# Spreading layers 1 and 2 of a group over 1.9 groups of differences, and writing the sorted degrees behind the differences of a PSUM tile

## The chip, the cores and the metric

The kernel runs on one core of one Trainium2 chip. A core has a matrix engine (TensorE, PE in the profile; its weight loads are listed as PEld), a vector engine (DVE), an activation engine (ACT), a general engine (POOL) and a queue that issues transfers (SP). The metric is the device time of one execution in microseconds, lower is better. Matmul results land in PSUM, which has eight banks of 512 fp32 values in each of 128 partitions.

## What is computed

The input is 128 graphs of 128 nodes with 64 features each, and a dense weighted adjacency matrix for each graph, about one entry in eight of it non-zero. Four layers follow each other. Each normalises the features, takes the positive part and adds what its block gives.

```
layer 0:  h[j,k] = relu(x[j] W1a + (x[j] - x[k]) W1b + b1)      for each edge j,k
          x += (sum over k of h[j,k]) W2 + degree[j] * b2
layer 1:  three times  h = relu(adj (h W + b)),  then  x += h Wout + bout
layer 2:  y = (adj h + h) W + b, each row divided by its norm,
          then normalised over all graphs and nodes (mean, variance), x += relu(y)
layer 3:  m = adj h;  x += tanh([h, m] W1 + b1) W2 + b2
```

Layer 0 is the large one: a difference and a positive part of 192 columns for every edge.

## The kernel before

The graphs are worked in 32 groups of G = 4. For layer 0 the nodes of a graph are sorted by their number of neighbours, and the neighbours of a node are numbered. One **task of differences** handles one neighbour number of all nodes of a group: a one-hot matrix (`oh` or `ohn`, made by DVE at lines 542 and 547) picks the neighbour's projected features by matmul, and the result is added to what node j itself gives. A group has 20 tasks: 12 for near neighbours (4 matmuls each) and 8 for others (12 each, three bf16 parts), in a fixed order, all of 128x192.

A task goes round three engines. ACT fills a difference tile in PSUM with `psort`, the node's own part (`fill`, line 561). PE adds the differences to it (line 569; every matmul is recorded under line 103). DVE adds the positive part to an accumulator in SBUF (lines 580 and 584; one task of a group, line 582, is ACT's). There are three difference tiles, `blks[0]` to `blks[2]`, of two banks each, and task t uses tile t mod 3. A tile's two banks have 512 columns each, of which 384 are used by differences. The columns behind them hold, in tiles 0 and 1, sums for layer 2 (`ysum`, `ysq`). The other two banks are a pool, from which every other matmul result takes one by turns (`bank`).

Beside the differences of group g two other kinds of work are woven in, written as Python generators that yield between steps:

- `prepare(g + 1)`: transposes the adjacency, numbers neighbours, sorts nodes (`lower`, `fro`, `to`, `to_b`), projects the features (`q`), stores and reloads them in another layout, and makes `psort`. It computes the degree of each node and the number of neighbours beyond the near ones (`degs`, two columns of bf16), and sorts them with four matmuls into tile `ps_deg` (lines 495 to 498). DVE makes `empty` and `spare_n` from it (lines 510 and 511); ACT uses `empty` in line 526, and `spare_n` is read at the end.
- `after_layer0(g - 1)`: the end of layer 0 (`layer0_end`: `ps_sA`, `ps_sB`, `ps_o`), `layer1` (a chain of `ps_ah`, `ps_ag`, `ps_pr` with a copy by ACT between each two) and the first half of `layer2_norm` (`ps_ga`, `ps_pr`, then norms, and sums over nodes into `ysum`). For group 29 it ends with `first_mean`, a mean over the groups so far; line 773 then subtracts it from `ys` of every group.

What sets the order of the work is a plan at build time. Each generator is held with the number of its units (15 and 26), the number done, and the number of groups that it lasts: 0.8 for `prepare`, `LASTS` = 1.5 for `after_layer0`. After each half of a task the plan takes the generator that is most behind, and steps it while there is budget:

```
late, s = max(((s[2] * s[3] / (nyields * s[4]) - s[1], s) for s in side), key=lambda k: k[0])
if late <= 0 or (spent["us"] >= budget and late < LAG):
    break
```

`s[2]` are the units, `s[3]` the halves of tasks since its start, `nyields` the 40 halves of a group, `s[4]` the groups that it lasts. `spent` is the plan's own guess of PE's time and `PACE` what it allows for half a task. With 1.5, `after_layer0` of two groups are in work at once in the first half of each group, and one alone in the second half. What is not done when the last group's differences end (`side[0][0]`) is stepped in turn with the last group's own `after_layer0`. The framework that records the program then orders each engine's instructions and sets the waits, so an engine's order is close to the written one, but not the same. It sets waits on a PSUM tile so that instructions of different engines on it come one after the other.

Of the kernel before, what the change touches and what calls it, by code (L numbers as in the profile page):

```python
# [20 lines left out]
G = 4  # L21
# [26 lines left out]
N_PREPARE, N_AFTER = 15, 26  # L48
PACE, LAG = 0.88, 2.5
LATE = 18  # L50
LASTS = 1.5
PARTS = [2, 4, 6, 6, 6, 8]
AHEAD = 3
NBLK = 3
W = NP * H0


@with_exitstack
def tile_adj_preln_d4(ctx: ExitStack, tc: tile.TileContext, io, out: bass.AP):
    nc = tc.nc  # L60
    const = ctx.enter_context(tc.tile_pool(name="const", bufs=1))
    over = const.tile([1, 1], I32, name="over")
    with ExitStack() as inner:
        network(inner, tc, io, out, over=over)
    more = nc.values_load(over, min_val=0, max_val=P)
    with tc.If(more > 0):
        x1 = nc.dram_tensor("x1_dram", [io["x"].shape[0] // G, P, G, F], F32, kind="Internal").ap()
        with ExitStack() as inner:
            dense_layer0(inner, tc, io, x1)
        with ExitStack() as inner:  # L70
            network(inner, tc, io, out, x1=x1)


def network(ctx, tc, io, out, over=None, x1=None):
# [7 lines left out]
    NG = B // G  # L82
# [10 lines left out]
    def spend(w, n, dtype):  # L93
        f32 = dtype == F32
        kind = (f32, tuple(w.shape), n)
        m = w.shape[-1]
        one = max(0.026, 0.00043 * n) if not f32 else max(0.22, 0.0018 * n) * (0.5 if m == F and n == P else 1.0)
        spent["us"] += one + (0.045 if kind != spent["kind"] else 0.0)
        spent["kind"] = kind

    def matmul(o, w, x, **kw):
        spend(w, math.prod(x.shape[1:]), x.dtype)
        return nc.tensor.matmul(o, w, x, **kw)  # L103
# [111 lines left out]
    where, at = {}, 0  # L215
# [31 lines left out]
    blks = [ps_blk.tile([P, 1024], F32, tag=f"blk{i}", name=f"blk{i}") for i in range(NBLK)]  # L247
# [3 lines left out]


    ysum, ysq = (t.rearrange("p (a n) -> p a n", a=2)[0:G, :, W:512] for t in blks[0:2])
    for t in (ysum, ysq):
        nc.vector.memset(t, 0.0)


# [25 lines left out]
    def bank(name):  # L283
        return ps.tile([P, 512], F32, tag="ps", name=name)
# [116 lines left out]
    def prepare(g):  # L401
# [6 lines left out]
        a = loaded.pop(g)  # L408
# [18 lines left out]
        degs = edge.tile([P, G, 2], BF16, tag="degs", name="degs")  # L427
# [33 lines left out]
        to_b = once.tile([P, G, P], BF16, tag="to_b", name="to_b")  # L461
# [30 lines left out]
        for q in range(3):  # L492
            nc.sync.dma_start(near_n[g % 2][q * THIRD : (q + 1) * THIRD].rearrange("r t b n -> r t (b n)"), n_dram[g].rearrange("(t r) c -> r t c", t=3))
        yield
        pd = bank("ps_deg")
        for b in range(G):
            matmul(pd[:, 2 * b : 2 * b + 2], to_b[:, b, :], degs[:, b, :], start=True, stop=True)
        pdv = pd[:, 0 : 2 * G].rearrange("p (b q) -> p b q", q=2)

        num_r = edge.tile([P, G, P], BF16, tag="num_r", name="num_r")  # L500
        for i in range(LIKE):
# [1 line left out]
        m, n = len(SEGS) - LIKE, SEGS[LIKE]  # L503
# [194 lines left out]
    def after_layer0(g):  # L698
        if x1 is None:
            yield from layer0_end(g)  # L700
        else:
            nc.sync.dma_start(xs[g], x1[g])
            save_transposed(g, load_adj(g))
        yield
        yield from layer1(g)
        yield from layer2_norm(g)
        if g == NG - 3:
            first_mean()
# [8 lines left out]
    else:  # L717


        run(prepare(0))  # L720
        per = len(tasks) // NG
        nyields = 2 * per
# [7 lines left out]
        for g in range(NG):  # L730
            if g:
                side.append([after_layer0(g - 1), 0, N_AFTER, 0, LASTS])
            if g + 1 < NG:
                side.append([prepare(g + 1), 0, N_PREPARE, 0, 0.8])
            for t in range(g * per, (g + 1) * per):
                for _ in differences(t):
                    budget += PACE
                    for s in side:
                        s[3] += 1
                    while side:  # L740
# [3 lines that stand above are left out]
                        step = next(s[0], "end")  # L744
                        s[1] += 1 if step is None else step if step != "end" else 0
                        if step == "end":
                            side.remove(s)
                    budget = min(budget, spent["us"] + PACE)
            if g + 1 < NG:
                assert len(side) <= 1  # L750
# [115 lines left out]
    parts, at = [], 0  # L866
# [183 lines left out]
```

## Time and profile before

| | us |
|---|---|
| median of three runs | 1437.3 (1434.69 to 1447.62) |
| profiled execution | 1441.81 |
| its span, first to last instruction | 1440.0 |
| DVE, closing a task (line 584), 576 times | 545.8 busy, 951 ns each |
| ACT, filling a tile (line 561), 544 times with `psort`, 96 with `psort_r` | 437.4 and 77.6 busy, 808 ns each |
| PE, difference matmuls, 3072 and 1536 | 325.9 and 203.6 busy |

The profile is one execution, taken by the hardware profiler. "Busy" of an engine is the time in which at least one of its instructions was running; matmuls are pipelined, so that a matmul of 248 ns is followed by the next after 82 ns, and PE's busy time holds such tails. Line numbers are those of the kernel before. A group of instructions is named by its line, the tile that it writes and those that it reads, with buffer numbers left out: `blk<-q,oh` is a difference matmul. A wait is put down to the instruction that ended it.

The start takes about 79 us (group 0 has to be prepared before anything else), groups 1 to 31 end at 1279.6, and the rest is the end of layer 2 and all of layer 3.

### The profile page before, as it was taken

How to read it: one execution, taken by the hardware profiler on the slowest of the kernel's cores; microseconds unless marked ns; L12 is line 12 of the kernel's file. 1: busy time of each engine (PE TensorE's matmuls, PEld its weight loads, DVE VectorE, ACT ScalarE, POOL GpSimd, SP SyncE). 2: the span in 40 equal slices, each digit the busy share in tenths (PEclk: the TensorE clock that was granted, in tenths of full speed). 3: DMA queues.
4: the chain of work that ended last, by engine and by line, in shares of the span. 5: the costliest groups of instructions: out<-in, count | busy, mean ns of one | idle time of the engine just before them, and what ended most of it. 6: DMA issues, size and time to landing. Idle time of an engine off the chain costs nothing.

```text
span 1440.0 us, 29446 instructions
## 1 busy us (share of the span) xinstructions
PE 1278.7 (89%) x11124; PEld 981.7 (68%) x11124; DVE 1197.9 (83%) x2691; ACT 1004.1 (70%) x1883; POOL 175.4 (12%) x258
## 2 busy tenths in 40 slices
PE   3788999999999999999999999999999999995788
PEld 1567777777777777777777777776777777763566
DVE  7788888888888888888888888888888888874983
ACT  1677777777777777777777777777677777862783
POOL 3000000000000000000000000000000000003930
PEclk9799999999999999999999999999999999997899
DMA  4543222222222222222222222222222222200345
GB/s 106 132 111 89 66 81 81 80 76 79 80 73 73 78 70 71 68 59 81 81 81 74 80 74 80 73 73 71 60 63 78 74 73 73 74 9 8 82 118 128
DMA packets 108788, 110.97 MB, mean 77 GB/s; under 512 B 42895, under 2 KB 88220, under 8 KB 108636
## 3 DMA queue, kind: packets, MB, share of 16 engines
q1 hardware_dynamic: 108636, 109.00, 28.0%
q8 instruction: 89, 1.46, 0.4%
q14 instruction: 63, 0.52, 0.1%
HBM read 52.70 MB, written 35.29 MB: 61 GB/s over the span
## 4 chain that ended last, share of the span: by engine, by line
PE 63%; DVE 20%; ACT 13%; issue 4%; DMA 0%; POOL 0%; DVEq 0%; ACTq 0%; POOLq 0%
PE blk L103 22%; PE ps_pr L103 10%; PE ps_ag L103 7%; DVE acc L584 5%; PE ps_p L103 5%; ACT blk L561 5%; PE ps_ga L103 4%; PE ps_sB L103 2%; PE ps_q L103 2%; PE ps_sA L103 2%; PE ps_ah L103 2%; PE ps_hm L103 2%; PE ps_to L108 2%; DVE lower L441 1%; DVE fro L451 1%
## 5 line engine op out<-in xcount | busy, mean ns | idle before, releaser
L584 DVE SCALAR_TENSOR_TENSOR acc<-blk,acc 128x768 f32<-128x768 f32 x576 | 545.8, 951 | 133.6 <-PE blk L103 91.2
L561 ACT COPY blk<-psort 128x768 f32<-128x768 f32 x544 | 437.4, 808 | 122.0 <-DVE acc L584 115.1
L103 PE MATMUL blk<-q,oh 128*128 128x192 bf16 x3072 | 325.9, 248 | 27.3 <-ACT blk L561 21.4
L103 PEld LDWEIGHTS <-oh 128*128 128x128 bf16 x3072 | 261.0, 98 | 55.5 <-issue 52.4
L103 PE MATMUL blk<-near_q,ohn 128*128 128x192 bf16 x1536 | 203.6, 247 | 10.9 <-ACT blk L561 9.3
L103 PEld LDWEIGHTS <-ohn 128*128 128x128 bf16 x1536 | 129.8, 98 | 64.1 <-issue 41.1
L642 POOL TENSOR_TENSOR x<-x,t 128x256 f32<-128x256 f32 x32 | 23.7, 741 | 529.2 <-DVE t L641 512.7
L103 PEld LDWEIGHTS <-ones_b 3*128 3x128 bf16 (+2 forms) x312 | 29.1, 93 | 74.3 <-issue 67.6
L561 ACT COPY blk<-psort_r 128x768 f32<-128x768 f32 x96 | 77.6, 808 | 0.7 <-DVE acc L584 0.7
L103 PE MATMUL ps_pr<-g,dT 128*128 128x128 f32 x512 | 74.0, 287 | 0.0
L103 PEld LDWEIGHTS ps_pr<-g,dT 128*128 128x128 f32 x512 | 62.0, 191 | 15.1 <-issue 15.1
L103 PE MATMUL ps_ag<-adjT,msg 128*128 128x128 f32 x512 | 71.9, 283 | 0.1
L542 DVE TENSOR_SCALAR ohn<-near_n 128x1536 bf16<-128x1536 bf16 x128 | 70.6, 555 | 0.0
L103 PEld LDWEIGHTS ps_ag<-adjT,msg 128*128 128x128 f32 x512 | 62.1, 191 | 5.2 <-ACT msg L635 2.3
L298 ACT ACTIVATE sq<-xc 128x256 f32<-128x256 f32 x96 | 40.1, 417 | 32.1 <-DVE xc L295 32.1
L627 ACT ACTIVATE dT<-ps_ag 128x512 f32<-128x512 f32 x96 | 56.9, 593 | 3.4 <-PE ps_ag L103 2.1
L103 PE MATMUL ps_p<-wp,hs 128*128 128x384 f32 x128 | 59.1, 544 | 0.0
L103 PE MATMUL ps_sA<-fro,acc 128*128 128x128 f32 x256 | 53.7, 292 | 3.5 <-DVE acc L584 2.5
L103 PE MATMUL ps_q<-wq,hT 128*128 128x384 f32 x128 | 52.6, 535 | 4.2 <-ACT hT L325 1.1
L103 PE MATMUL ps_hm<-ident,h 128*64 128x128 f32 x248 | 41.8, 299 | 14.0 <-ACT h L841 14.0
L668 POOL TENSOR_TENSOR y<-y,nrm 128x256 f32<-128x256 f32 x32 | 19.8, 619 | 276.9 <-PE blk L103 261.2
L526 ACT ACTIVATE extra<-psort,empty 128x192 f32<-128x192 f32 x128 | 51.2, 450 | 0.0
(221 smaller groups left out, 2610.8 us busy)
## 6 DMA issues: line engine op xcount, KB each, us to landing
q_dram<-q SPq DMA_DIRECT2D x32, 567.0 KB
near_q<-q_dram SPq DMA_DIRECT2D x96, 189.0 KB
near_n<-n_dram SPq DMA_DIRECT2D x96, 126.0 KB
a<-in_adj_dram SPq DMA_DIRECT2D x32, 256.0 KB
adjT_dram<-adjT SPq DMA_DIRECT2D x32, 256.0 KB
adjT<-adjT_dram SPq DMA_DIRECT2D x32, 256.0 KB
psort_r<-psort SPq DMA_DIRECT2D x32, 228.0 KB
fro_r<-fro SPq DMA_DIRECT2D x32, 152.0 KB
```

The costliest lines, as they stand in the source:

```text
L103: return nc.tensor.matmul(o, w, x, **kw)
L108: return nc.tensor.transpose(o, x, i)
L298: nc.scalar.activation(sq, xc, AF.Square)
L441: nc.vector.tensor_tensor(lower, pk.rearrange("p (b n) -> p b n", n=P), key.unsqueeze(2).to_broadcast([P, G, P]), ALU.is_lt)
L451: nc.vector.tensor_scalar(flat(fro), pl, place_p, None, ALU.is_equal)
L526: nc.scalar.activation(of(extra, b), of(psort, b), AF.Relu, scale=empty[:, g, b : b + 1])
L542: nc.vector.tensor_scalar(oh.rearrange("p t b n -> p (t b n)"), near_n[g % 2].rearrange("p t b n -> p (t b n)"), float(i + 1), None, ALU.i ...
L561: nc.scalar.copy(columns(t), psorts[g][in_segments(n)])
L584: nc.vector.scalar_tensor_tensor(acc, o, 0.0, acc, ALU.max, ALU.add)
L627: nc.scalar.activation(flat(dT), pa, AF.Relu)
L642: nc.gpsimd.tensor_tensor(xt, xt, t, ALU.add)
L668: nc.gpsimd.tensor_tensor(y, y, over_f(nrm), ALU.mult)
```

## The change

The number of groups over which `after_layer0` is spread goes from 1.5 to 1.9. And the sorted degrees no longer take a bank of the pool: they are written into the columns behind the differences of tile 2, at a place of their own for each group (8 columns; 16 groups in each of the tile's two banks). Those columns are set to zero once, and the matmuls add to that instead of starting afresh (`start=False`). Nothing else changes.

```diff
-LASTS = 1.5
+LASTS = 1.9
...
     ysum, ysq = (t.rearrange("p (a n) -> p a n", a=2)[0:G, :, W:512] for t in blks[0:2])
-    for t in (ysum, ysq):
+    degs_at = blks[2].rearrange("p (a n) -> p a n", a=2)[:, :, W:512]
+    for t in (ysum, ysq, degs_at):
         nc.vector.memset(t, 0.0)
...
-        pd = bank("ps_deg")
-        for b in range(G):
-            matmul(pd[:, 2 * b : 2 * b + 2], to_b[:, b, :], degs[:, b, :], start=True, stop=True)
-        pdv = pd[:, 0 : 2 * G].rearrange("p (b q) -> p b q", q=2)
+        half, at = divmod(g, NG // 2)
+        pd = degs_at[:, half, at * 2 * G : (at + 1) * 2 * G]
+        for b in range(G):
+            matmul(pd[:, 2 * b : 2 * b + 2], to_b[:, b, :], degs[:, b, :], start=False, stop=True, skip_group_check=True)
+        pdv = pd.rearrange("p (b q) -> p b q", q=2)
```

## The prediction

> **What bounds the kernel now.** First the busy shares of the page: no engine is full on average.
>
> ```profile
> PE 1278.7 (89%) x11124; PEld 981.7 (68%) x11124; DVE 1197.9 (83%) x2691; ACT 1004.1 (70%) x1883; POOL 175.4 (12%) x258
> ```
>
> The span is 32 groups of 20 tasks of differences, then an end. The DVE instruction that closes a task is the one of lines 580 and 584, so the ends of these cut a group into four stretches of five tasks. The busy times of three groups in a row, four stretches each (start:end us, length, busy us of PE, PEld, DVE, ACT, POOL, clock, DMA):
>
> ```profile
> 544.22:557.19 12.97, 11.49 (x109) 9.16 (x107) 12.80 (x27) 6.41 (x11) 2.11 (x3) 1.00 0.13 43
> 557.19:564.31 7.12, 6.26 (x55) 4.57 (x54) 6.72 (x15) 6.22 (x15) 0.61 (x1) 1.00 0.12 37
> 564.31:572.52 8.21, 7.77 (x72) 5.79 (x72) 7.58 (x21) 6.60 (x11) 0.61 (x1) 1.00 0.26 88
> 572.52:582.98 10.46, 10.46 (x83) 8.13 (x82) 6.36 (x13) 9.20 (x18) 0.00 (x0) 1.00 0.57 131
> 582.98:595.64 12.66, 11.05 (x106) 8.95 (x105) 12.54 (x27) 6.36 (x12) 2.07 (x3) 1.00 0.13 44
> 595.64:603.33 7.69, 6.70 (x61) 4.87 (x58) 7.32 (x17) 6.80 (x15) 0.61 (x1) 1.00 0.13 36
> 603.33:613.83 10.50, 9.89 (x79) 6.85 (x80) 8.99 (x27) 8.88 (x16) 0.61 (x1) 1.00 0.32 95
> 613.83:622.77 8.94, 8.72 (x81) 7.46 (x78) 6.58 (x13) 8.04 (x15) 0.73 (x1) 1.00 0.49 122
> 622.77:634.52 11.75, 10.30 (x98) 8.47 (x99) 11.29 (x24) 5.45 (x10) 1.34 (x2) 1.00 0.14 46
> 634.52:642.16 7.64, 6.80 (x62) 4.97 (x60) 7.02 (x16) 6.41 (x15) 0.61 (x1) 1.00 0.12 35
> 642.16:650.46 8.30, 8.15 (x71) 5.95 (x70) 7.45 (x21) 6.67 (x12) 0.61 (x1) 1.00 0.21 64
> 650.46:660.75 10.29, 10.29 (x82) 8.02 (x81) 6.36 (x13) 9.06 (x18) 0.00 (x0) 1.00 0.61 151
> ```
>
> Means over the three groups, stretches 1 to 4: length 12.46, 7.48, 9.00, 9.90 (38.84 a group); DVE 12.21, 7.02, 8.01, 6.43 (33.67); PE 10.95, 6.59, 8.60, 9.82; ACT 8.77 in the fourth. So the bound changes within a group: the first quarter is DVE's (98% busy), the fourth PE's (99%, DVE 65%). A group loses 5.2 us of DVE, nearly all in the second half, where DVE waits for PE. The waits on DVE from 544.22 to 660.75 (total us, times, longest) say so:
>
> ```profile
> DVE acc L584 <- PE blk L103: 8.9, 10, 1.5
> DVE acc L584 <- ACT extra L526: 1.8, 3, 0.6
> DVE acc L584 <- ACT psort L518: 1.3, 1, 1.3
> ```
>
> Busy PE overstates work, so I price matmuls by the distance between starts in the timeline (start, length, what):
>
> ```profile
> 692.64 1.15 PE L103 MATMUL blk<-q,oh 128*128 128x192 bf16 x12
> 693.73 0.39 PE L103 MATMUL ps_pr<-rows,ones_b 3*128 3x512 bf16 x1
> 694.04 1.16 PE L103 MATMUL ps_pr<-g,dT 128*128 128x128 f32 x8
> 695.04 0.49 PE L103 MATMUL blk<-near_q,ohn 128*128 128x192 bf16 x4
> ```
>
> Twelve differences take 1.09 us (82 ns each within a run), the bias row 0.31, eight fp32 passes 1.00 (112 ns within a run).
>
> The old home of the degrees, tile ps_deg, held nobody up by much (who waited for it):
>
> ```profile
> L103 PE MATMUL ps_deg<-degs,to_b x128: 163/163/169, 36.7 to 1234.4; 128*128 128x2 bf16 x128
> ...
>   PEld L103: 0.7, 1
>   PE ps_p L103: 0.6, 1
> ```
>
> **What the Trainium skill says.** The Trainium skill, "Perfetto Trace Analysis", Optimization Strategy: where the most contended engine changes over time, interleaving the regimes may help. The trace agrees that there are two regimes (98% DVE, 99% PE); that interleaving them pays is open. The Trainium skill, same page, Identifying the Most-Contended Engine: busy matmul time is a poor measure of distance to the limit, busy time of DVE a fair one. The table agrees: PE shows 10.95 of 12.46 us in a stretch that DVE rules. The Trainium skill, "PSUM — Partial Sum Buffer", PSUM bank collisions: two engines must not touch one bank in the same 32 partitions at once, not even at different columns. In the kernel before the degrees had a bank to themselves, so no row shows such an order for them. The Trainium skill, same page, Engine vs sequencer instructions: matmuls start and complete in program order, so all of PE's queue stands behind a waiting one; the trace has PE at a standstill behind single waits (0.6 us for fro at line 451), which agrees.
>
> **Part 1: LASTS from 1.5 to 1.9.** No instruction is removed or added; steps of layers 1 and 2 come later. In the instruction order of the two programs I counted what stands between the same task ends, in the three group patterns that repeat, and multiplied by their durations in the trace of before. DVE instructions overlap by some ns: rows sum to 38.5 us a group where DVE is busy 33.7, so I scale by 0.875.
>
> DVE, rows per group by stretch: before 13.8, 8.0, 9.7, 6.9; after 11.3, 9.2, 9.3, 8.7. From the first stretch go, per group, mean and xc of a layernorm (409 + 416 ns), 1.3 of an h (417 to 483 ns), a third of a var (409), 0.7 each of an rstd (170) and a t (418), one ohn (555) and fro at line 451 (742), whose chain now ends later; 2.3 one-hots (283) come in. The second gains fro, one mean and xc and one t, and loses nrm; the fourth gains two ohn and the small nrm and counted steps (about 160 ns each). Scaled: -2.2, +1.1, -0.3, +1.5 us.
>
> PE side work by start distances: before 4.95, 3.74, 4.32, 4.22; after 4.49, 4.80, 5.23, 2.84. The two ag stages (16 fp32 passes, 1.8 us) leave the fourth for the first, sB and the last pr go from the first to the second, zT's ps_ga from the second to the third. ACT by the same count stays: 6.1, 5.3, 7.4, 8.7 before; 6.7, 4.9, 7.3, 8.6 after.
>
> Stretch by stretch: the first is DVE's and loses 2.2, to 10.2 (PE's 2.95 us of differences, 36 of them by 82 ns, and 4.49 of side work stay below). In the second both engines gain 1.1: 8.6. The second half is PE's: side work falls from 8.54 to 8.07, 0.5 less of 18.9; DVE's 15.6 there (14.4 + 1.2) still fits. Sum -2.2 + 1.1 - 0.5 = -1.6 us a group.
>
> Not all of that comes. Where both engines are near full each waits for the other: in the second stretch now (DVE 7.02, PE 6.59) the length is 7.48, 0.46 over the larger. The first and last stretch of after are new ones of that kind (last: ACT 8.6, DVE 7.6, PE by then below). I charge 0.4 for each: -0.8 us a group. With three difference tiles PE can't run more than about three tasks ahead; if I take the larger of PE, DVE and ACT over running windows of tasks instead of five-task stretches, windows of four give -0.7, of five -1.0, of three +0.4. So the unknown runs from +0.4 to -1.6, and I take -0.8. Groups 2 to 30 are 29 full ones: -23 us.
>
> The ends: when the differences of group 31 are through, its predecessor's layers have 12.3 of 26 units left instead of 8.7. And the mean that line 773 subtracts comes after group 29's sums, now 0.9 of a group into group 31 instead of 0.5: by the orders 15 of the 32 passes of line 773 (416 ns, 6.2 us) stood inside group 31, now none. Group 31 takes 32.8 us with PE and DVE busy 30.4 each; DVE's part falls by over 6, PE's stays, so I take 2 us back there. From its end at 1279.6 to 1314.0 the chain of group 31's own layers sets the time, with about 18 us of PE work, 13 of DVE and 18 of ACT behind the last task, which become 19.9, 18.7 and 20.2; the rest of group 30's layer 1 stands between the sA matmuls on PE. I take +3. Net +1 (-2 to +4).
>
> **Part 2: the degrees.** Same four matmuls (26 ns apart, 0.1 us), same two DVE reads (215 + 210 ns): nothing saved there. The one memset more is a DVE pass of 128x256 (411 to 418 ns where such passes have rows) in the start, where PE waits for rows until 19 us. One of two free banks is no longer held by ps_deg: the two waits above, 1.3 us in the whole run, are the most this can give by itself. New: the four matmuls and both reads must come between two uses of difference tile 2, either after its fill and before its differences, or after its acc and before its fill. The order shows both. Queued behind: on PE the next differences of that tile wait for spare_n; in the other pattern ACT's fill waits for it, and behind it the copy of ah, for which ps_ag waits. The hold is 0.1 + 0.43 us and the handovers, and with the fill (808 ns) behind it 1.4 us; what PE has in between is pr, p and ah matmuls, 1.9 to 2.1 us by the distances above. Taken: 0, between 0 and +1 us a group if that cover is gone (DVE late at num_r, which stands in front of the read). Below nothing by 1.3 us in all. POOL's to_b, which the matmuls read, is ready long before (it sits idle 169.8 us of the span for its input). On SP's queue one thing moves: the first load of near_n now stands ahead of q's store, and it waits for n's store to land; in the timeline of before such loads are issued 2.7 us after that store (686.18, 688.88), and their first readers come at 701, so some 10 us cover this.
>
> **Sum.** The profiled execution took 1441.81 us (1440.0 of span and 1.8 around it); -23 +1 makes 1419.8. The median of the three runs is 4.5 us lower, 1437.3; the same difference gives 1415.
>
> **Rivals.** A: the full balance is reached, -1.6 by 29 + 1 = -45, 1392. For it: DVE's row sums are nearly even after. Against: lumps of PE work (sB and pr in two neighbouring tasks). B: no change within 1%: the windows of three are the right measure for a part of the group, or ACT, with 8.6 us of the last stretch, takes PE's place there so that stretch 4 falls little; -0.2 a group and the end, 1432. C, slower: the hold on tile 2. If DVE reaches empty and spare_n 1 us late, PE, in order, stands before the next differences of tile 2, and then loses the two-task lead it needs; 0.8 us over 31 groups is +25, against a balance that yields nothing: 1462, or 1455 with a quarter of the gain. It decides from 0.8 us a group on. For it: the read stands behind five num_r steps and, in one pattern, a reduction; against: the cover of 1.9 us.
>
> **Chances.** Forecast 0.47, A 0.13, B 0.22, C 0.18. One per cent (14 us) is about what a measurement can tell here from no change. Faster by more: forecast and A, less a little of the forecast's edge: 0.58; within: 0.23; slower: 0.19. Range: down to A's 1392, up to 1446, which leaves out most of C and little else.
>
> **What would show it.** Right: first stretch near 10.5 us, fourth near 9, DVE idle under 4.5 us a group, waits of acc for PE halved. Part 2 wrong: PE rows waiting for spare_n, or fills of tile 2 with idle before them. Part 1 wrong: the first stretch shortens but the second and third grow by as much, with DVE waiting for PE there and PE for fills. The forecast fails if PE and DVE take turns at a finer grain than three tiles can bridge.

## The result, and the profile after

| | before | after |
|---|---|---|
| median, 20 runs each | 1439.9 (1434.69 to 1447.62) | 1430.28 (1426.15 to 1436.79) |
| ratio | | 0.9932, 95% interval 0.9917 to 0.9947 |
| profiled execution / its span | 1441.81 / 1440.0 | 1435.94 / 1434.1 |

The change made the kernel 9.7 us faster, where 22 were forecast: right in sign, less than half in size, and within the 1% of the prediction's rival B. The line of busy shares in the page of the kernel after:

```profile
PE 1251.2 (87%) x11124; PEld 983.2 (69%) x11124; DVE 1186.8 (83%) x2692; ACT 997.8 (70%) x1883; POOL 179.5 (13%) x258
```

PE's and DVE's shares have hardly moved (89% and 83% before). The same cut as in the prediction, five tasks at a time by the ends of the DVE instructions that close them (now lines 582 and 586), gives this for one group in the middle of the run (start:end us, length, busy us of PE, PEld, DVE, ACT, POOL, clock, DMA), and its last line sums this group and its two neighbours:

```profile
734.84:747.46 12.62, 11.76 (x117) 10.09 (x115) 9.68 (x21) 6.85 (x12) 1.39 (x3) 1.00 0.15 48
747.46:756.72 9.26, 8.10 (x72) 6.89 (x71) 8.14 (x16) 6.35 (x13) 1.34 (x2) 1.00 0.10 30
756.72:765.57 8.85, 7.74 (x73) 5.49 (x71) 8.05 (x23) 8.16 (x16) 0.00 (x0) 1.00 0.37 111
765.57:773.54 7.97, 7.91 (x65) 5.90 (x64) 7.74 (x17) 7.14 (x16) 0.88 (x1) 1.00 0.48 123
...
sum 115.11, PE 104.59 PEld 83.14 DVE 99.95 ACT 85.29 POOL 10.41; mean PE 8.72 PEld 6.93 DVE 8.33 ACT 7.11 POOL 0.87
```

DVE's load is even now, 9.7, 8.1, 8.1 and 7.7 us where it was 12.2, 7.0, 8.0 and 6.4. The lengths are not: the first stretch is as long as ever, and DVE stands still for 2.9 us of it. Over the groups 2 to 30 of both traces the mean lengths are (the last column is the forecast, with its 0.4 us of friction in the first and in the last stretch):

| stretch | before | after | difference | forecast |
|---|---|---|---|---|
| 1 | 12.53 | 12.36 | -0.17 | -1.8 |
| 2 | 7.58 | 9.28 | +1.70 | +1.1 |
| 3 and 4 | 8.99 + 9.91 | 8.67 + 8.37 | -1.86 | -0.1 |
| a group | 39.01 | 38.68 | -0.33 | -0.8 |

Twenty-nine groups by -0.33 are -9.6 us. The start took 2.2 us more, group 1 took 2.3 less, group 31 took 1.1 more and what follows it 2.7 more; together -5.9, the difference of the two spans. (The medians differ by more than these two executions.) The means hold a few groups in which TensorE's granted clock dips, 4 of the 29 before and 3 after. At full clock, 1.00 in all four stretches, every third group is alike to within some hundredths of a us nearly throughout; the medians of these three patterns, averaged, are 38.84 us a group before and 38.38 after, -0.46.

Where the time of the first two stretches goes is in the waits of the same three groups, first DVE's, then PE's (what waited, for what; total us, times, longest):

```profile
DVE acc L586 <- PE blk L103: 4.7, 6, 1.5
DVE acc L582 <- PE blk L103: 3.0, 3, 1.4
DVE t L643 <- PE ps_pr L103: 2.2, 3, 0.7
...
PE ps_to L108 <- DVE fro L452: 3.5, 3, 1.2
PE blk L103 <- ACT blk L563: 3.4, 5, 0.8
```

Both lists hold waits of 0.7 to 1.5 us that come once in each group. The timeline of the group above (start, length, what; idle time before it in brackets) shows them in order:

```profile
736.43 0.96 DVE L582 SCALAR_TENSOR_TENSOR acc<-blk,extra 128x768 f32<-128x768 f32 x1 [0.39 <-PE blk L103]
737.73 1.16 PE L103 MATMUL ps_pr<-g,dT 128*128 128x128 f32 x8
739.34 0.96 DVE L586 SCALAR_TENSOR_TENSOR acc<-blk,acc 128x768 f32<-128x768 f32 x1 [1.54 <-PE blk L103]
740.23 1.08 PE L103 MATMUL ps_ag<-adjT,msg 128*128 128x128 f32 x8
741.51 0.96 DVE L586 SCALAR_TENSOR_TENSOR acc<-blk,acc 128x768 f32<-128x768 f32 x1 [1.01 <-PE blk L103]
...
745.24 0.68 DVE L442 TENSOR_TENSOR lower<-ps_key,key 128x512 bf16<-128x512 f32 x1
745.49 0.82 PE L103 MATMUL blk<-q,oh 128*128 128x192 bf16 x8 [0.83 <-ACT blk L563]
746.24 0.45 PE L103 MATMUL ps_sB<-fro,acc 128*64 128x128 f32 x4
...
747.52 1.10 PE L103 MATMUL ps_pr<-gout,dT 128*128 128x64 f32 x8
748.46 0.38 PE L103 MATMUL ps_place<-lower,ones_b 128*128 128x512 bf16 x1
748.66 0.42 DVE L643 TENSOR_TENSOR t<-ps_pr,nm 128x256 f32<-128x256 f32 x1 [0.74 <-PE ps_pr L103]
749.87 0.74 DVE L452 TENSOR_SCALAR fro<-ps_place,place_p 128x512 f32<-128x512 f32 x1
750.67 0.66 PE L108 MATMUL ps_to<-ident,fro 128*128 128x128 f32 x4 [1.16 <-DVE fro L452]
```

From 736 to 742 PE works through sA, a pr, the rest of sA and an ag, and DVE stands before three tasks, 2.94 us in all. From 742.39 DVE has its sorting passes (`rank_t`, `leftT`, `key`, `rank`, `lower`) and runs without a gap; the fill of the next tile waits for a task that stands behind the first of them, and PE stands 0.83 us. PE is then late with sB and the pr for `t`, DVE waits 0.74 for `t`; `fro` stands behind `t` and one more task, and PE waits 1.16 for `fro`. The two engines take turns.

### The profile page after: what moved, and what is told of

Read it like the earlier page. It is cut to its first block, busy times and chain, and to the rows that moved or that the text cites. A ratio compares the mean times of both kernels' runs of the same rounds, so it can differ in the third digit from the quotient of the medians.

```text
span 1434.1 us, 29471 instructions
## 1 busy us (share of the span) xinstructions
PE 1251.2 (87%) x11124; PEld 983.2 (69%) x11124; DVE 1186.8 (83%) x2692; ACT 997.8 (70%) x1883; POOL 179.5 (13%) x258
## 5 line engine op out<-in xcount | busy, mean ns | idle before, releaser
L103 PE MATMUL blk<-q,oh 128*128 128x192 bf16 x3072 | 333.6, 247 | 35.2 <-ACT blk L563 34.3
L103 PE MATMUL blk<-near_q,ohn 128*128 128x192 bf16 x1536 | 196.2, 247 | 8.9 <-ACT blk L563 8.0
L670 POOL TENSOR_TENSOR y<-y,nrm 128x256 f32<-128x256 f32 x32 | 24.4, 762 | 600.2 <-DVE acc L586 329.3
L637 ACT COPY msg<-ps_pr 128x512 f32<-128x512 f32 x64 | 37.3, 584 | 42.5 <-PE ps_pr L103 28.3
L484 POOL TENSOR_TENSOR db<-degs,b_all 128x256 f32<-128x256 bf16 x32 | 19.7, 615 | 366.9 <-DVE degs L429 366.9
L103 PE MATMUL ps_p<-wp,hs 128*128 128x384 f32 x128 | 62.1, 568 | 0.0
L582 DVE SCALAR_TENSOR_TENSOR acc<-blk,extra 128x768 f32<-128x768 f32 x32 | 30.6, 958 | 35.4 <-PE blk L103 34.8
L108 PE MATMUL ps_to<-ident,fro 128*128 128x128 f32 x128 | 21.9, 296 | 37.3 <-DVE fro L452 37.3
L605 ACT COPY sB<-ps_sB 128x256 f32<-128x256 f32 x32 | 11.9, 372 | 60.8 <-PE ps_sB L103 60.8
```

The costliest lines, as they stand in the source:

```text
L108: return nc.tensor.transpose(o, x, i)
L484: nc.gpsimd.tensor_tensor(db, over_f(degs[:, :, 0]), over_g(b2_all), ALU.mult)
L582: nc.vector.scalar_tensor_tensor(acc, o, 0.0, psorts[g][2], ALU.max, ALU.subtract)
L605: nc.scalar.copy(flat(sB), pB[:, 0 : NP * P])
L637: nc.scalar.copy(flat(msg), pm)
L670: nc.gpsimd.tensor_tensor(y, y, over_f(nrm), ALU.mult)
```

## The experiments

Times are medians; each ratio is against runs of the kernel before on the same chip (1437.2 to 1439.9), with its 95% interval.

### Each half of the change alone

`e1_spread_only`, the kernel before with the new spreading and its degrees in `ps_deg`:

```diff
-LASTS = 1.5
+LASTS = 1.9
```

> The kernel before with LASTS 1.9 alone; the degrees stay in their own bank. Theory 1 (the spreading gives the whole gain, and it is small because in the changed kernel the first five tasks of a group are now PE's): about 1430, like the changed kernel. Theory 2 (the spreading gives the 22 us that were forecast, and the hold on tile 2 takes half of them back): 1417 to 1422. Theory 3 (the gain is that of the bank that the degrees gave free): 1440, like before.

`e2_degrees_only`, the kernel after with the old spreading:

```diff
-LASTS = 1.9
+LASTS = 1.5
```

> The changed kernel with LASTS back at 1.5; only the degrees are moved. Theory 1: 1440, within 3 us of before. Theory 2 (the hold costs about 0.4 us a group): 1450. Theory 3: 1430.

Measured: e1 1457.54, ratio 1.0128 (1.0106 to 1.0150), slower by 19; e2 1433.09, ratio 0.9966 (0.9952 to 0.9979), faster by 5. None of the three theories had e1 slower, and e2 lies between theories 1 and 3. The parts don't add: 19 - 5 is not -10. With the new spreading the degrees' place is worth 27 us. In the waits of e1 over the whole run stands one that the kernel after lacks:

```profile
PE ps_p L103 <- ACT sqy L656: 19.2, 29, 0.7
PEld ps_p L103 <- issue: 31.5, 64, 0.8
```

Its place in the timeline of e1:

```profile
733.94 0.39 ACT L656 ACTIVATE sqy<-ps_pr 128x256 f32<-128x256 f32 x1
734.38 0.32 PE L103 MATMUL ps_p<-rows,ones_b 3*128 3x384 bf16 x1 [0.66 <-ACT sqy L656]
```

The pool's two banks go round. With `ps_deg` between, the turn that `ps_p` gets is the bank from which ACT reads `ps_pr` twice (`y` and `sqy`), 0.66 us on PE in each of 29 groups. By this count the 19.2 us of it would be most of the 27, but a wait is not yet time lost, and how much of the 27 it carries wasn't tested; the weight loads of `ps_p` wait 31.5 in e1 against 12.0 in the kernel after, but that is partly the same time.

### Is it the bank, or the tile behind which the degrees lie?

`e5_degrees_behind_hs`: 1.9, and the degrees in eight unused columns of the bank that `ps_ga` of `hs` takes anyway; no bank of their own, no turn of difference tile 2. The two reads follow at once.

```diff
-        hs = gathered(h, to, "hs")
+        ph = bank("ps_ga")
+        pd = ph[:, NP * P : NP * P + 2 * G]
+        for b in range(G):
+            matmul(pd[:, 2 * b : 2 * b + 2], to_b[:, b, :], degs[:, b, :], start=True, stop=True)
+        hs = gathered(h, to, "hs", pt=ph)
...
-        pd = bank("ps_deg")
```

> LASTS 1.9 as in the changed kernel, but the degrees lie behind hs in the pool bank that hs has anyway (columns 256 to 263), and empty and spare_n are made right after. So ps_deg takes no bank of its own, and tile 2 has no hold either. The spreading alone gave 1457.5, both changes 1430.3. Theory A (the 27 us between them are the pool's bank: with ps_deg in the pool ps_p has to wait until ACT has emptied ps_pr, 0.7 us on PE and 0.8 us on its weight loads in each group): about 1430, within 6 us. Theory B (they come from the place of the matmuls in PE's order or from tile 2 as a place, not from the bank): nearer to 1457 than to 1430.

Measured: 1423.71, ratio 0.9895 (0.9876 to 0.9914). That is on the side of theory A, a little faster than its 1424 to 1436. So what mattered was that the degrees take no bank of the pool, not that they lie in tile 2; the turn on tile 2 costs some us if anything (6.6 between the two kernels, though the matmuls and the reads move in the order too). A turn of the pool with nothing in it wasn't tried.

### Is DVE's idle time in the first stretch slack?

Two more DVE passes of 128x512 beside the sorting passes, before (`e3_before_more_dve`) and after (`e4_after_more_dve`); their result is not used.

```diff
+        junk = once.tile([P, G, P], BF16, tag="junk", name="junk")
+        for _ in range(2):
+            nc.vector.scalar_tensor_tensor(flat(junk), flat(rank_t), float(NEAR), flat(mT), ALU.min, ALU.add)
```

> The kernel before with two more DVE passes of 128x512 in every prepare, right after the degrees are copied, that write a tile which nobody reads: 2 by 0.68 us as the rank passes of that shape take, some 1.2 us a group of added DVE time in the first five tasks. There DVE is 98% busy, so all theories expect nearly all of it: 31 by 1.2 is +37, about 1477.

> The same two DVE passes in the changed kernel. Theory 1 (PE rules the first five tasks now and DVE has 2.7 us of idle there): +0 to +12 on the changed kernel, 1430 to 1442. Rival (DVE's chain of sorting steps still sets the first stretch, which is why it did not shorten): +37, 1467.

Measured: e3 1502.67, ratio 1.0434 (1.0401 to 1.0467); e4 1513.56, ratio 1.0512 (1.0486 to 1.0538), 83 above the kernel after. The first of the two passes took 0.68 us and the second 1.03 (medians of 32 each in e4); by the distance of starts the pair takes 1.56 us of DVE, so 31 groups of it are 48. These run times can't be compared with the others as they are: TensorE's mean clock was lower in these two profiles (e3 0.954, e4 0.937, against 0.973), and it dips in 21 and 17 of the groups 2 to 30. Two groups of e4 of the same pattern, stretches 1 and 2 of each, the first with dips and the second without (columns as above), show what a dip does:

```profile
652.02:666.19 14.17, 12.71 (x117) 11.08 (x117) 11.23 (x23) 6.81 (x11) 1.69 (x3) 0.92 0.18 55
666.19:677.96 11.77, 10.28 (x75) 8.55 (x71) 8.36 (x17) 6.43 (x13) 1.34 (x2) 0.81 0.08 23
903.08:917.25 14.17, 12.41 (x123) 10.61 (x121) 11.23 (x23) 7.12 (x12) 1.69 (x3) 1.00 0.14 44
917.25:926.25 9.00, 7.50 (x67) 6.36 (x66) 8.14 (x16) 6.15 (x13) 1.34 (x2) 1.00 0.10 29
```

The mirror of it: half of sA's matmuls done a second time, eight fp32 passes by 112 ns or 0.9 us of PE in a group, after (`e6_after_more_pe`) and before (`e7_before_more_pe`).

```diff
+            for acc, f, start in sums if b % 2 else ():
+                nc.tensor.matmul(pA[:, b * P : (b + 1) * P], of(acc, b, slice(0, P)), f[:, b, :], start=start, stop=not start)
```

> The changed kernel with half of the ps_sA matmuls done twice (8 fp32 passes of 112 ns more, 0.9 us a group in the first five tasks; the plan's guess of PE's time is left as it was). Theory C (in the changed kernel PE and DVE take turns in the first stretch: first three tasks wait for PE's lumps of ag, pr and sA, the next two for DVE's sorting passes, so that each added piece counts in full): 31 by 0.9, +28, about 1458. Theory D (DVE's chain of sorting passes alone sets the stretch): +0 to +9, at most 1439.

> The same doubled matmuls in the kernel before, where DVE was 98% busy in that stretch and PE had 1.5 us of idle. Theories C and D both: mostly covered, +0 to +14, 1439 to 1453. If it costs +28 the first stretch of the kernel before was not DVE's alone either, and the forecast's starting point falls.

Measured: e6 1463.45, 33 above the kernel after; e7 1463.56, 26 above the kernel before, outside the +0 to +14 of both theories. Only groups at full clock compare all six kernels (medians of each of the three patterns, averaged, us):

| stretch | before | e3, DVE +1.56 | e7, PE +0.9 | after | e4, DVE +1.56 | e6, PE +0.9 |
|---|---|---|---|---|---|---|
| 1 | 12.46 | 13.48 | 13.16 | 12.35 | 13.90 | 13.27 |
| 2 | 7.48 | 7.48 | 7.06 | 9.26 | 9.00 | 9.26 |
| 3 | 9.00 | 9.00 | 9.83 | 8.52 | 8.52 | 8.52 |
| 4 | 9.90 | 9.90 | 8.87 | 8.24 | 8.30 | 8.24 |
| a group | 38.84 | 39.86 | 38.93 | 38.38 | 39.72 | 39.29 |
| such groups, of 29 | 25 | 8 | 20 | 26 | 12 | 24 |

In the kernel after, PE's added 0.9 counts in full (+0.9), which refutes theory D, and of DVE's 1.56 there come 1.3, 41 us in 31 groups, which refutes theory 1 (the rest of e4's 83 goes with the dips); in the first stretch alone both count in full. DVE's 2.9 us of standing there absorb nothing: the two engines stand in one chain, PE's piece and DVE's piece one after the other. In the kernel before, DVE's passes cost 1.0 of 1.56, and PE's matmuls next to nothing over the group (+0.1), as a stretch that is DVE's would have it. But e7 shifted the order as well (stretch 3 +0.8, stretch 4 -1.0), and its first stretch did grow by 0.7, so e7 tells less. Of the 21 us by which e7's profiled execution is longer, groups 2 to 30 hold 12.6, with dips in 9 groups against 4, group 31 holds 7.2, and what follows it 2.3.

### A smaller step

`e8_after_1p8`, the kernel after with

```diff
-LASTS = 1.9
+LASTS = 1.8
```

> The changed kernel with LASTS 1.8 in place of 1.9; the degrees behind tile 2. If the balance over a group sets the time, which LASTS changes little by little (DVE rows by stretch 9.6, 11.0, 9.5, 8.4 and PE side work 3.8, 5.0, 5.3, 3.3 us by the same count as in the prediction): within 6 us of the changed kernel, 1424 to 1436. If the accidents of the order set it, more than 10 us away on either side.

Measured: 1393.55, ratio 0.9700 (0.9679 to 0.9721), 37 us below the kernel after, by a tenth of a group. Its four stretches in one group, in the columns as above, and the sum of three groups:

```profile
712.74:721.40 8.66, 8.54 (x87) 7.59 (x87) 8.13 (x14) 5.20 (x9) 1.91 (x3) 1.00 0.19 60
721.40:731.83 10.43, 8.60 (x79) 6.92 (x78) 9.61 (x20) 6.69 (x13) 0.73 (x2) 1.00 0.10 29
731.83:740.39 8.56, 8.34 (x77) 5.89 (x76) 8.11 (x23) 7.95 (x16) 0.00 (x0) 1.00 0.34 105
740.39:749.73 9.34, 9.34 (x79) 7.27 (x77) 7.24 (x19) 8.45 (x17) 0.61 (x1) 1.00 0.52 128
...
sum 110.91, PE 103.79 PEld 82.66 DVE 100.16 ACT 85.19 POOL 10.02; mean PE 8.65 PEld 6.89 DVE 8.35 ACT 7.10 POOL 0.83
```

A balance that changes little by little, within 6 us of the kernel after, is refuted. PE and DVE do the same work as after (103.8 and 100.2 against 104.6 and 100.0 in three groups) in 4.2 us less. In the order of 1.8 the pr that stood in the same task as sA lies two tasks earlier, and the last pr lies two tasks earlier than in 1.9, one task ahead of sB instead of beside it.

### Which of the two meetings costs: sA beside pr, or the sorting beside sB and pr?

`e11_1p9_sort_later`, the kernel after with the preparation spread over 0.84 of a group in place of 0.80, which moves its sorting passes, and its other steps, by half a task to a task:

```diff
-                side.append([prepare(g + 1), 0, N_PREPARE, 0, 0.8])
+                side.append([prepare(g + 1), 0, N_PREPARE, 0, 0.84])
```

> The changed kernel, LASTS 1.9, with one thing moved: the preparation's steps are spread over 0.84 of a group instead of 0.80, so that its sorting passes (rank_t, leftT, key, lower, rank, degs, fro) come half a task to a task later and no longer stand in one row of five beside the matmuls of sB and pr. The full pile of sA and pr in the second task stays. No instruction is added or removed. Theory P (the pile of sA and pr in one task starves DVE, whatever the sorting does): within 8 of 1430. Theory S (the row of sorting passes stands where PE needs DVE for its next tile, and then sB and pr come late for t): 1395 to 1415. Theory of the even balance over five tasks: within 4 of 1430.

`e12_after_1p85`, the kernel after with

```diff
-LASTS = 1.9
+LASTS = 1.85
```

> The changed kernel with LASTS 1.85. In its order pr no longer stands beside sA in the second task (as with 1.8), but the second half of a first stretch has sB, place, to and o in one pile in the seventh task (heavier than with 1.9). Theory P (pile of sA and pr): 1390 to 1402. Theory S (sorting passes beside a pile of sB and pr): between, or as slow as 1.9: 1412 to 1432. A smooth dependence on LASTS would give 1408 to 1416.

Measured: e11 1407.99, ratio 0.9787 (0.9763 to 0.9810); e12 1400.18, ratio 0.9733 (0.9709 to 0.9757). Moving the preparation alone took 22 us off, with the pile of sA and pr left in its place, so theory P fails here; in e12 theory S fails. Neither is enough by itself, and the even balance, which said no more than 4, falls. That the meeting with the sorting costs is shown by e11. That the pile costs by itself is not shown by e12: its last pr moved two tasks ahead as well, so that the waits of `t` and `fro` below fell there too (to 13 and 8 times). And in e11, with the pile in place, DVE's waits for the tasks' matmuls fell from 87.3 us to 39.7. The first stretch fell from 12.36 to 10.85 us in e11; in e12 it stayed at 12.26, and the second fell from 9.28 to 7.99. What went in e11 is a pair of waits. Over the whole run, first in the kernel after:

```profile
PE ps_to L108 <- DVE fro L452: 37.3, 32, 1.8
DVE t L643 <- PE ps_pr L103: 30.7, 32, 8.0
```

and in e11:

```profile
DVE t L643 <- PE ps_pr L103: 9.5, 3, 8.0
PE ps_to L108 <- DVE fro L452: 4.9, 4, 1.8
```

They came in all 32 groups, and are left in three or four. (The kernel before had 19.9 us of the first and 15.4 of the second, that in nine groups only.) In the order of e11 sB runs ahead of `ps_key`, and the pr for `t` while DVE is still among the sorting passes, so that `t` finds it done. How much of the 37 us between 1.9 and 1.8 each meeting carries by itself isn't settled: the edits also move some layernorm steps of the second half of a group.

### The two other places of the degrees at 1.8

`e9_before_1p8`, the kernel before (`ps_deg`) with `LASTS` 1.8, and `e10_1p8_behind_hs`, the edit of e5 with `LASTS` 1.8.

> The kernel before with LASTS 1.8 alone: the degrees keep their own tile ps_deg in the pool of two banks. With the degrees behind the differences, 1.8 gave 1393.6. Bank theory (a third user of the two banks makes ps_p wait for an ACT copy whenever layers 1 and 2 are spread, about 0.9 us in each of 29 groups): 1412 to 1422. Rival (the loss of 1.9 alone, +18.7, was an accident of that one order and the degrees' place is worth no more than the 5 us it gave at 1.5): 1393 to 1401.

> LASTS 1.8 with the degrees in unused columns of the bank that ps_ga of hs holds anyway, so that neither a bank of their own nor a turn of difference tile 2 is taken. Bank theory: as fast as 1.8 with the degrees behind the differences or a little faster, as at 1.9 (there 6.6 us less): 1384 to 1395. Rival (what counts is where each step falls in the order, and a move of the two reads by a task is enough to change it): away from 1393 by 10 or more.

Measured: e9 1403.38, ratio 0.9747 (0.9726 to 0.9769); e10 1385.17, ratio 0.9637 (0.9605 to 0.9669). With all the combinations:

| degrees in | 1.5 | 1.8 | 1.85 | 1.9 |
|---|---|---|---|---|
| a bank of their own | 1439.9 | 1403.4 | | 1457.5 |
| columns behind the differences | 1433.1 | 1393.6 | 1400.2 | 1430.3 |
| columns behind hs | | 1385.2 | | 1423.7 |

The place of the degrees has the same sign in every column, and its size depends on the order: 5 to 10 us at 1.5 and 1.8, 27 at 1.9. At 1.8 the bank costs 10, less than the bank theory's least (18) and 2 more than the rival's most, and the wait of `ps_p` for `sqy` isn't in the trace of e9; DVE's waits for the tasks' matmuls are longer by 5.7 us instead (79.0 against 73.3, all closing instructions together). What makes them longer is open. e10 is the fastest kernel of this study, 55 us below the kernel before and 45 below the changed one.

## Why the prediction was right or wrong

**Stretch 1, "-2.2 to 10.2": wrong, and this is the step that failed.** DVE's busy time there fell by 2.6 us, a little more than counted, but the length by 0.17. The sentence "PE's 2.95 us of differences, 36 of them by 82 ns, and 4.49 of side work stay below" cut PE's work at the ends of PE's own tasks. PE works one to three tasks ahead of DVE, so in the time of DVE's first stretch it does other things: in the group 734.84 to 747.46 these are 48 differences and 69 other matmuls (ag, aT, sA, pr, ag, rank, key and sB), PE is 11.76 us busy of 12.62, and it is shown waiting only once, 0.83 us. The prediction's own table had the warning, PE 10.95 busy in a stretch for which 7.9 of work were counted, and put it down to tails of matmuls. Experiment e6 shows that PE's work counts there now (+0.9 us for 0.9), and e4 that DVE's does too. In the kernel before the stretch was DVE's in the main: e7's added PE work cost 0.1 us a group at full clock, though its order shifted as well. What failed is the count of what the new order puts there.

**The friction, "0.4 for each": mis-sized.** It was charged to the first and the last stretch. In the first it was right in kind and a fifth of what came: -2.2 by count became -0.17, 2.0 us lost where 0.4 was charged. The second stretch, which was charged nothing, grew by 0.6 more than counted. In the first and at the start of the second, each engine waits for the other once or twice a group (DVE 2.94 and 0.74, PE 0.83 and 1.16 in the group shown). This is what the prediction named as its way to fail: turns at a finer grain than three tiles can bridge. It had the mechanism, and gave it too small a price. Its windows of five tasks gave -1.0 a group and those of three +0.4; the truth, -0.33, lies midway.

**Stretch 2, "+1.1 to 8.6": right in direction, 0.6 short.** It took 9.28, of which the wait for `t` and the one for `fro` are a part.

**"The second half is PE's": half right.** The fourth stretch is: PE's count fell by 1.38 there and the length by 1.54. The third isn't: PE's count rose by 0.91 and the length fell by 0.32, as DVE's did by count (-0.3). So the gain came where 0.1 was expected. The first stretch is off by 1.6 us, the second by 0.6, and the second half by 1.8 the other way; that the total per group is off by no more than 0.5 is luck.

**The ends: +3 after group 31 was right (+2.7), -2 within it was not (+1.1).**

**Part 2, "1.3 us in the whole run are the most this can give by itself": wrong.** By itself it gave 5 us (3 to 7), and with the new spreading 27. The bound was read from waits for `ps_deg` in the old order. But a bank in a pool taken by turns sets who gets which bank after it; in the new order that puts `ps_p` behind ACT's two reads of `ps_pr`. The forecast had no row for this, and was saved by it: of the two parts the spreading alone, which was to bring all of the gain, made the kernel slower by 19. That the sign came out right is luck.

**Rival C, the hold on tile 2: not seen.** PE's waits for `spare_n` come to 0.5 us in the whole run. e5, without that hold, was 6.6 faster, so a small cost isn't excluded. Rival A, the full balance, is refuted by the first stretch. Rival B, within 1%, is where the time lies: its -0.2 us a group is near the -0.33, and its first reason, windows of three for a part of the group, points the right way. Its second doesn't hold: the fourth stretch fell by 1.5, ACT didn't take PE's place.

**What should have shown it.** First stretch near 10.5: no, 12.4. Fourth near 9: 8.4. DVE idle under 4.5 us a group: no, (115.11 - 99.95) / 3 = 5.05 against 5.2 before. Waits of acc for PE halved: no, 87.3 us against 95.9 in the whole run.

The Trainium skill, "Perfetto Trace Analysis", Optimization Strategy, says that interleaving may help where the most contended engine changes over time. The prediction left open whether it pays. These runs say that it can (-36 us for 1.8 with nothing else changed) and that it can cost (+19 for 1.9): evening out the sums is not enough, since what an engine does next must not hang on what the other does now.

## What to carry to other kernels

Before you read a gain from evened sums, count the work of both engines over the same stretch of time, not each by its own tasks, and look in the timeline for pairs of waits, A for B and then B for A, once in every round: they put the two engines' work in series, whatever the sums say. Where a planner places the work, try its neighbours: here a tenth of a group in one constant was worth four times the change under study. A buffer that nobody is seen waiting for can still decide, by its turn in the pool, who waits for the next one; so an intermediate result that fits into unused columns of a bank already held is worth trying there: with 1.8 it took 18 us off here (1403.4 to 1385.2). And before you subtract two run times, look at the granted clock of each stretch.

## What the runs showed of the hardware

The two added DVE passes of e4 are alike, 128x512 of bf16 from SBUF to SBUF, and yet in nearly every group the first took 0.68 us and the second 1.03:

```profile
744.10 0.68 DVE L432 SCALAR_TENSOR_TENSOR junk<-rank_t,mT 128x512 bf16<-128x512 bf16 x1
745.57 1.04 DVE L432 SCALAR_TENSOR_TENSOR junk<-rank_t,mT 128x512 bf16<-128x512 bf16 x1
```

The second stood behind a task's closing and began while an addition of POOL (`x<-x,db`, 0.72 us) had been running for 0.24 us. Which of these made it longer, if either, wasn't tested.

The granted clock isn't even within a run. In a group of the kernel before (columns as above) it dips for a part of two stretches; the third line is the dip alone, 3.41 us at half clock:

```profile
699.50:712.16 12.66, 11.05 (x101) 8.94 (x100) 12.54 (x27) 6.23 (x11) 2.07 (x3) 0.97 0.14 44
712.16:721.29 9.13, 8.21 (x65) 6.18 (x62) 7.31 (x17) 6.92 (x15) 0.61 (x1) 0.86 0.10 29
711.32:714.73 3.41, 3.41 (x22) 2.96 (x24) 2.69 (x5) 1.39 (x3) 0.61 (x1) 0.50 0.23 68
```

The lost clock is half of 3.41, 1.7 us, and that group is 1.4 us longer than others of its pattern. Such a dip is five times the gain per group that the change brought (0.33), so one group is a poor measure of an edit, and so is a median when most groups dip, as in e3 and e4; groups at full clock are a better one.

The dips don't seem to fall by chance. The four among groups 2 to 30 of the kernel before begin within 0.4 us after PE had waited 0.63 us for `fro`. In e4 this wait took 1.49 us in the group at 652.02 and the one for a fill 1.43, and dips came in 17 groups. But most groups of the kernel before have the wait and no dip, and no run changed the waits alone; so it isn't shown that they bring the dips on.
